# Two-layer interaction network: leftover products of layer 1 in batches of eight, other load times, a fifth operand buffer, and X5 and X4 behind X3 and X1

## The chip, the core and the metric

The kernel runs on one core of a Trainium2 chip. TensorE (PE in the profile, with its weight loads as PEld) multiplies matrices, VectorE (DVE), ScalarE (ACT) and GpSimd (POOL) do elementwise work, and SyncE (SP) and ACT issue transfers (DMA). The metric is the time of one execution in device microseconds (us). The kernel before took 2045.23 us, the median of five runs from 2044.97 to 2048.3.

## The reference

For each of 4096 rows there is x with 32 fields and 16 embedding places. A layer forms all products of its input's fields with the fields of x at each place, weighs them into 128 outputs, adds a bias and normalises each output over all rows and places.

```python
def _cin_layer(out, x, W, b, gamma, beta):
    h = jnp.einsum('rne,rfe->rnfe', out, x).reshape(r, -1, e)
    h = jnp.einsum('rce,oc->roe', h, W) + b[None, :, None]
    return _batchnorm(h, gamma, beta)

h1 = _cin_layer(x, x, W1, b1, g1, beta1)            # 32*32 products -> 128
out, direct1 = (h1[:, :64], h1[:, 64:])
direct2 = _cin_layer(out, x, W2, b2, g2, beta2)     # 64*32 products -> 128
return jnp.concatenate([direct1, direct2], axis=1).sum(axis=-1)
```

Everything is float32. The means and variances of layer 1 are needed before layer 2 can begin.

## The kernel before

**Sites and tiles.** A site is one row at one embedding place; there are 65536. They are cut into 128 tiles of 512 sites. Layer 1 goes tile by tile; layer 2 goes by 64 chunks, each of two tiles side by side.

**Layer 1, the products.** In layer 1 the product of fields i and j is the same as that of j and i, so 528 different products are enough. For each tile `load_main` (L282) loads two operands, a and b, of 512 KB each, and one VectorE instruction (`multiply_main`, L384) makes the products z, 128 partitions by four blocks of 512. TensorE weighs them in four matmuls with 128 partitions each (L428). Sixteen products are left over per tile, of fields that stand 16 apart. Those of eight tiles (a *group*, `GROUP`) are packed into one tile zr of 128 partitions: `load_rem` (L275) loads r, 512 KB per group, and `leftovers` (L371) multiplies. `add_leftovers` (L376) weighs them: four matmuls of 32 partitions each, one for each of four tiles, which use four different row strips of the array and so run at the same time. The 32 partitions of a strip hold the leftovers of two tiles; the weights at index 4 or 5 of `w1_sb` are zero on the other tile's rows. So zr serves two batches of four.

**Order in layer 1.** In the loop over 124 tiles (L401) a batch of leftovers stands ahead of the main matmuls of each tile t that is a multiple of four; it begins the accumulation of tiles t to t+3. Only the first batch comes after tile 1 and ends tiles 0 and 1. Below, *s* is t modulo 8. r is loaded at s = 4 and multiplied at s = 0. A finished tile goes through `finish` (L342), one tile late: ScalarE copies all 128 rows with the bias to e, rows 0 to 63 to `kept` (which goes to DRAM as layer 2's input h) and rows 64 to 127 to `ed`; VectorE takes statistics of e (L115) and, every second tile, sums ed (L364).

**Buffers.** a and b have four buffers each (`lpool`), z has four (`zpool`), r and zr have one each (`rpool`), PSUM has six banks for accumulators (`psum`) and two for small results and layer 2's factors (`factors`). The loads of tile t+4 wait until VectorE has multiplied tile t, and z of tile t+4 waits until TensorE is done with tile t.

**Side work of layer 1** hangs on tile numbers in the list `EARLY` (L205): every 24 tiles x of 16 chunks is loaded in two halves (`load_x`, L187, with a stride through the array xb), ScalarE negates two pieces, VectorE forms four pieces of differences (L199) and the result goes to DRAM. Layer 2's first operands are loaded at tiles 75 (b), 83 (bx) and 91, 99, 107 and 115 (a). The weights w2 are loaded at tile 6; `combine_weights` (L319) forms sums of them on VectorE.

**The end of layer 1.** The last four tiles (`ENDING`) are weighed in two halves of 64 outputs (L461): first the half that layer 2 needs for its statistics, then the other, while VectorE and ScalarE work out the scale and shift (L505 to L519, L537).

**Layer 2** takes each chunk in four stages of a form of Strassen's algorithm: seven products of blocks in place of eight. VectorE forms two products of a stage (L667), `multiply(z[:, 0::3], f1, b)` and then `multiply(z[:, 1:3], f2, bx)`, and one sum (t2); GpSimd forms a sum (L703) and two differences (t1 and t4 in one instruction, L714). A stage has fourteen matmuls, two at a time on the two halves of the columns, in the methods `x2`, `x54`, `x31` and `x67` of `Stage`. x54 needs GpSimd's differences and is taken one stage late: the loop (L856 on) issues x2, then x54 of the stage before (`waiting`), then x31 and x67.

**What sets the order.** The order on each engine is that of the program for layer 2 (`queue` chains the instructions) and, for layer 1, that of a scheduler which moves instructions of different tiles past each other within their dependencies. SP issues its loads in a fixed order: one that waits holds all behind it.

Of the kernel before, what the change touches and what calls it, by code (L numbers as in the profile page):

```python
# [38 lines left out]
FP = mybir.dt.float32  # L42
AF = mybir.ActivationFunctionType
ALU = mybir.AluOpType
AX = mybir.AxisListType

P = 128
# [3 lines left out]
T = 512  # L51
NC = HALF // T
NT = 2 * NC
# [3 lines left out]
WRAP = 48  # L57
# [10 lines left out]


@with_exitstack  # L70
def tile_cin(ctx: ExitStack, tc: tile.TileContext, xa, xb, xr, w1, w1m, w2, bn, out):
    nc = tc.nc

    const = ctx.enter_context(tc.tile_pool(name="const", bufs=1))
# [89 lines left out]
    def load_a(c, i):  # L164

        a = apool.tile([P, 2 * T], FP, tag="a", name="a")
        nc.sync.dma_start(a, hs[c][16 * i : 16 * (i + 1), :].unsqueeze(1).to_broadcast([16, 8, 2 * T]))
        return a

    def load_b(c):  # L170

        b = bpool.tile([P, 4, T], FP, tag="b", name="b")
        at = xb.offset + 2 * c * WRAP * T
        nc.sync.dma_start(b, bass.AP(xb.tensor, at, [[0, 16], [4 * T, 8], [1, 4 * T]]))
        return b
# [10 lines left out]

    def load_x(g, k):  # L187

        at = xb.offset + ((2 * DIFF * g + 1) * WRAP + 2 * k) * T
        nc.sync.dma_start(xs[:, k], bass.AP(xb.tensor, at, [[2 * WRAP * T, DIFF], [4 * T, 8], [1, 2 * T]]))  # L190

    def negate(part):
        x = xs[:, 0, part * T : (part + 1) * T]
# [10 lines left out]

    EARLY = []  # L205
    for g in range(NC // DIFF):
        at = 14 + 24 * g
        EARLY += [(at + 2 * k, lambda g=g, k=k: load_x(g, k)) for k in range(2)]
        EARLY += [(at + 12 + 2 * k, lambda k=k: negate(k)) for k in range(2)]
        EARLY += [(at + 16 + 2 * k, lambda k=k: difference(k)) for k in range(4)]  # L210
        EARLY += [(at + 23, lambda g=g: store_difference(g))]
    early = []
    EARLY += [(75, lambda: early.append(load_b(0))), (83, lambda: early.append(load_bx(0)))]
    EARLY += [(91 + 8 * k, lambda i=i: early.append(load_a(0, i))) for k, i in enumerate(STAGES)]
    loads = []

    def loaded(c):
# [43 lines left out]
    ss1 = const.tile([P, 2], FP, tag="ss1", name="ss1")  # L261

    with ExitStack() as one:
        lpool = one.enter_context(tc.tile_pool(name="lpool", bufs=4))
        rpool = one.enter_context(tc.tile_pool(name="rpool", bufs=1))
        opool = one.enter_context(tc.tile_pool(name="opool", bufs=2))
        kpool = one.enter_context(tc.tile_pool(name="kpool", bufs=3))
# [1 line left out]
        zpool = one.enter_context(tc.tile_pool(name="zpool", bufs=4))  # L269
        wpool = one.enter_context(tc.tile_pool(name="wpool", bufs=1))  # L270

        xs = xpool.tile([P, 2, 2 * T], FP, tag="x", name="xs")
        xd = xpool.tile([P, 2 * T], FP, tag="xd", name="xd")

        def load_rem(g):  # L275
# [87 lines left out]
        def sum_direct(c):  # L363
# [4 lines left out]
                ALU.add,  # L368
            )

        def leftovers(r):  # L371
            zr = rpool.tile([P, T], FP, tag="zr", name="zr")
            nc.vector.tensor_tensor(zr, r[:, :T], r[:, T:], ALU.mult)
            return zr

        def add_leftovers(t, zr, begun=0):  # L376

            for k in range(4):
                rows = slice(32 * k, 32 * (k + 1))
                nc.tensor.matmul(  # L380
                    pss[t + k], w1_sb[rows, 4 + t % GROUP // 4, :], zr[rows, :], start=k >= begun, stop=k < begun
                )

        def multiply_main(z, a, b, k):  # L384

# [14 lines left out]
        r = load_rem(0)  # L400
        for t in range(NT - ENDING):  # L401
            s = t % GROUP
            if s == 4 and t + 4 < NT:
                r = load_rem(t // GROUP + 1)
            if FIRST <= t + 1 < NT:
                main.append(load_main(t + 1))
            if s == 0 and t > 0:
                zr = leftovers(r)
            z = zpool.tile([P, 2, 2, T], FP, tag="z", name="z")
            if t < FIRST:  # L410
                for k in range(2):
                    for j in range(2):
                        product = multiply_chunk(z, *main[0], k, j)
            else:

                for k in (slice(0, 1), slice(1, 2)) if t == FIRST else (slice(0, 2),):
                    product = multiply_main(z, *main[0], k)
            main.pop(0)
            if t == FIRST - 1:
                with tc.issue_after(product.ins):  # L420
                    zr = leftovers(r)
            if s % 4 == 0:
                for k in range(4):
                    pss[t + k] = psum.tile([P, T], FP, tag="ps", name="ps")
            if s % 4 == 0 and t > 0:
                add_leftovers(t, zr)
            for m in range(4):
                nc.tensor.matmul(  # L428
                    pss[t],
                    w1_sb[:, m, :],  # L430
                    z[:, m // 2, m % 2, :],
                    start=t < FIRST and m == 0,
                    stop=t >= FIRST and m == 3,
                )
            if t == FIRST - 1:
                add_leftovers(0, zr, FIRST)
            if t > 0 and t < ending - 1:
                evicted = finish(t - 1)
            if t == 20:
                combine_weights()  # L440
                b1_swapped = const.tile([P, 1], FP, tag="b1s", name="b1_swapped")
                for x, y in ((low, high), (high, low)):
                    nc.scalar.activation(b1_swapped[x], b1[y], AF.Identity)
            if t == 0:
                continue
            with tc.issue_after(loads[-1].ins), tc.issue_after(product.ins), tc.issue_after(evicted.ins):
                if t == 12:
                    nc.vector.tensor_reduce(spread, select.rearrange("k i n f -> k (n f) i"), AX.X, ALU.max)
                if t == 14:
                    nc.vector.tensor_reduce(block, select.rearrange("k i n f -> k i (n f)"), AX.X, ALU.max)  # L450
                if t == 6:
                    nc.sync.dma_start(w2_sb, w2)
                for at, load in EARLY:
                    if t == at:
                        load()
# [19 lines left out]
        def add_leftovers_halves(banks, zr, direct, begun):  # L475

            for k in range(ENDING):
                rows = slice(32 * k, 32 * (k + 1))
                to = banks[k][half_of[(k + direct) % 2]]
                matmul(to, w1_sb[rows, 5, half_of[direct]], zr[rows, :], k not in begun, k in begun)  # L480

        zs = []
        for k in range(ENDING):
            if k + 1 < ENDING:
                main.append(load_main(ending + k + 1))
            zs.append(zpool.tile([P, 2, 2, T], FP, tag="z", name="z"))
            queue("dve", lambda: multiply_main(zs[k], *main.pop(0), slice(0, 2)))

        with tc.issue_after(lasts["dve"].ins):
            for t in (ending - 2, ending - 1):  # L490
# [365 lines left out]
    for c in range(NC):  # L856
# [3 lines left out]
        for k, i in enumerate(STAGES):  # L860
# [37 lines left out]
            if c == k == 0:  # L898
                stage.ordinary()
            elif (c, k) == (NC - 1, 3):  # L900
                stage.at_last(waiting)
            else:
                stage.x2()
                if waiting:
                    waiting.x54()
                stage.x31()
                stage.x67()
            if c > 0 or k > 0:
                waiting = stage
# [99 lines left out]
```

## Time and profile before

| | |
|---|---|
| median of five runs | 2045.23 us |
| the profiled execution | 2044.97 us |
| its span, first to last instruction | 2043.2 us |
| TensorE busy | 2026.8 us, 99% |
| VectorE busy | 1959.4 us, 96% |
| GpSimd busy | 1486.8 us, 73% |
| ScalarE busy | 1185.7 us, 58% |
| first main matmul of layer 1 | at 8.19 us |
| first matmul of layer 2 | at 490.38 us |
| last matmul of layer 2 starts | at 2030.18 us |

In the lines of a profile L428 is line 428 of the program. A float32 matmul shows as two instructions. A timeline line gives start and duration in us, engine, line, operation, the tile written and the tiles read, the shapes, and the number of instructions merged in it; in square brackets stands the engine's idle time just before it, and what ended it. A busy TensorE is not a TensorE at its peak, since matmuls overlap; what counts is the distance between their starts.

### The profile page before, as it was taken

The page shows a single profiled execution, that of the slowest core. Times are in us where ns is not written, and L with a number is a line of the kernel's source. Part 1 is how long each engine was busy: PE and PEld are TensorE (multiplying, and loading weights), DVE is VectorE, ACT ScalarE, POOL GpSimd, SP SyncE. Part 2 cuts the span into 40 slices and gives each one's busy share as a digit, 9 for nine tenths or more (in the row PEclk, how much of TensorE's full clock was granted, in tenths as well). Part 3 has the DMA queues.
Part 4 walks back from the last instruction along what each step waited for, and adds up shares of the span by engine and source line. Part 5 has one row for each costly group of instructions (what it writes and reads, how often), then busy time and mean ns, then how long its engine had stood idle before and what let it go on. Part 6 is the DMA issues. An engine that isn't in the chain of part 4 may idle for free.

```text
span 2043.2 us, 24467 instructions
## 1 busy us (share of the span) xinstructions
PE 2026.8 (99%) x8500; PEld 863.5 (42%) x8500; DVE 1959.4 (96%) x1521; ACT 1185.7 (58%) x1914; POOL 1486.8 (73%) x525
## 2 busy tenths in 40 slices
PE   9999999999999999999999999999999999999997
PEld 3444444443334444444444444444444444444443
DVE  8998988988999999999999999999999999999998
ACT  4555555554566666655665656556656565566564
POOL 0000000002999999999999999999999999999996
PEclk9999999999999999999999999999999999999998
DMA  9999999996777777777776677777766777777661
GB/s 391 373 353 370 347 361 370 359 374 189 176 178 175 176 175 180 192 174 183 179 176 168 172 175 176 178 181 177 176 167 173 175 173 184 179 176 176 168 163 42
DMA packets 112380, 440.70 MB, mean 216 GB/s; under 512 B 13056, under 2 KB 13056, under 8 KB 103808
## 3 DMA queue, kind: packets, MB, share of 16 engines
q1 hardware_dynamic: 105840, 418.43, 73.1%
q10 hardware_dynamic: 6416, 20.72, 2.7%
q8 instruction: 66, 1.08, 0.2%
q14 instruction: 58, 0.48, 0.1%
HBM read 417.07 MB, written 22.02 MB: 215 GB/s over the span
## 4 chain that ended last, share of the span: by engine, by line
PE 97%; DVE 1%; DMA 1%; issue 0%; ACT 0%; POOL 0%; DVEq 0%; ACTq 0%; POOLq 0%
PE x L698 73%; PE ps L428 21%; PE ps L380 2%; PE ps L461 1%; DVE zz L667 1%; DMA b<-in_xb 0%; DMA w1m_sb<-in_w1m 0%; DVE zz L672 0%; POOL t L714 0%; ACT f L659 0%; DVE d L934 0%; ACT u L659 0%; DVE both L662 0%; ACT both L659 0%; POOL t L703 0%
## 5 line engine op out<-in xcount | busy, mean ns | idle before, releaser
L714 POOL TENSOR_TENSOR t<-zz,t 128x2048 f32<-128x2048 f32 (+1 forms) x260 | 1163.9, 4477 | 20.7 <-DVE t L662 0.8
L698 PE MATMUL x<-t,s_sb 128*64 128x512 f32 x2040 | 958.3, 592 | 0.5 <-POOL t L714 0.5
L698 PE MATMUL x<-zz,s_sb 128*64 128x512 f32 x2048 | 933.1, 592 | 0.0
L698 PE MATMUL x<-zz,w_sb 128*64 128x512 f32 x2056 | 758.6, 592 | 0.0
L703 POOL TENSOR_TENSOR t<-zz 128x512 f32<-128x512 f32 x255 | 327.0, 1282 | 516.2 <-DVE zz L667 515.9
L667 DVE TENSOR_TENSOR zz<-f,bx 128x2048 f32<-128x2048 f32 x255 | 581.9, 2282 | 19.5 <-ACT f L659 19.5
L659 ACT ACTIVATE f<-a,keep 128x512 f32<-128x512 f32 x512 | 398.2, 778 | 342.7 <-DVE zz L667 294.7
L667 DVE TENSOR_TENSOR zz<-f,b 128x2048 f32<-128x2048 f32 x255 | 581.9, 2282 | 0.1
L698 PEld LDWEIGHTS x<-t,s_sb 128*64 128x64 f32 x2040 | 279.0, 137 | 498.6 <-issue 469.5
L698 PE MATMUL x<-t,w_sb 128*64 128x512 f32 x1020 | 479.3, 592 | 0.0
L428 PE MATMUL ps<-z,w_sb 128*128 128x512 f32 x992 | 434.7, 596 | 2.0 <-POOL w_sb L312 1.8
L698 PEld LDWEIGHTS x<-zz,s_sb 128*64 128x64 f32 x2048 | 279.7, 137 | 253.9 <-issue 246.3
L387 DVE TENSOR_TENSOR z<-a,b 128x2048 f32<-128x2048 f32 (+1 forms) x127 | 288.1, 2270 | 42.4 <-PE ps L428 27.8
L428 PEld LDWEIGHTS ps<-z,w_sb 128*128 128x128 f32 x992 | 185.7, 190 | 248.9 <-issue 230.7
L698 PEld LDWEIGHTS x<-zz,w_sb 128*64 128x64 f32 x2056 | 235.8, 137 | 124.5 <-issue 122.3
L659 ACT ACTIVATE b<-zz 128x512 f32<-128x512 f32 x255 | 152.4, 598 | 187.1 <-DVE zz L667 187.1
L352 ACT ACTIVATE e<-ps,bn_sb 128x512 f32<-128x512 f32 x124 | 85.2, 687 | 218.4 <-PE ps L428 182.2
L662 DVE TENSOR_TENSOR t<-zz,b 128x512 f32<-128x512 f32 x255 | 173.0, 678 | 0.4
L698 PEld LDWEIGHTS x<-t,w_sb 128*64 128x64 f32 x1020 | 139.4, 137 | 0.0
L596 ACT ACTIVATE unread<-e,center 128x512 bf16<-128x512 f32 x122 | 86.2, 707 | 0.0
L358 ACT ACTIVATE ed<-ps,bn_sb 64x512 f32<-64x512 f32 x124 | 84.8, 684 | 2.3
L115 DVE BATCH_NORM_STATS2 stats<-e 128x6 f32<-128x512 f32 x124 | 84.8, 685 | 0.0
(103 smaller groups left out, 866.0 us busy)
## 6 DMA issues: line engine op xcount, KB each, us to landing
a<-h SPq DMA_DIRECT2D x256, 512.0 KB, 4.5
b<-in_xb SPq DMA_DIRECT2D x64, 1024.0 KB, 9.0
a<-in_xa SPq DMA_DIRECT2D x127, 512.0 KB, 7.5
b<-in_xb SPq DMA_DIRECT2D x127, 512.0 KB, 8.2
bx<-in_xb SPq DMA_DIRECT2D x64, 512.0 KB, 8.9
bx<-x SPq DMA_DIRECT2D x64, 512.0 KB, 10.5
h<-kept ACTq DMA_DIRECT2D x64, 256.0 KB, 5.7
r<-in_xr SPq DMA_DIRECT2D x16, 512.0 KB, 9.3
```

The lines of the kernel that those rows point to most:

```text
L115: nc.vector.bn_stats(self.stats[:, self.at, :], h)
L352: nc.scalar.activation(e, ps, AF.Identity, bias=b1)
L358: done = nc.scalar.activation(ed[to, :], ps[KEEP:, :], AF.Identity, bias=b1[KEEP:])
L387: return nc.vector.tensor_tensor(z[:, k], a.rearrange("p (a t) -> p a t", a=2)[:, k].unsqueeze(2).to_broadcast([P, n, 2, T]), b.rearrange( ...
L428: nc.tensor.matmul(pss[t], w1_sb[:, m, :], z[:, m // 2, m % 2, :], start=t < FIRST and m == 0, stop=t >= FIRST and m == 3,)
L596: return nc.scalar.activation(unread, e[:, s], AF.Square, bias=center[:, s], accum_out=squares[:, s, c : c + 1])
L659: return queue("act", lambda: nc.scalar.activation(to, source, AF.Identity, **scale_bias))
L662: return dve(lambda: nc.vector.tensor_tensor(to, x, y, ALU.add))
L667: dve(lambda: nc.vector.tensor_tensor(z, a, b.rearrange("p (k q) t -> p k q t", k=2), ALU.mult))
L698: queue("pe", lambda: nc.tensor.matmul(self.of[x], w, b, start=start, stop=stop))
L703: queue("pool", lambda: nc.gpsimd.tensor_tensor(t2[:, 0], z[:, 1, 0], z[:, 0, 0], ALU.add))
L714: queue("pool", lambda: nc.gpsimd.tensor_tensor(t14[:, k, q], z[:, 2 + k.start : 2 + k.stop, q], twice[:, k, q], ALU.subtract))
```

## The change

1. **Leftovers.** At s = 0 two batches stand behind each other: first that of the four tiles just finished (s = 4 to 7 of the group before), which it *ends*, then that of the four tiles to come, which it *begins*. zr now holds the leftovers of tiles 8k-4 to 8k+3, so r is packed anew (17 pieces in place of 16), is loaded at s = 1 (and at tile 3), and the last four tiles get a product of their own.
2. **Banks and evictions.** Tiles with s = 6 and 7 use the two banks of `factors`; `finish` comes four tiles late in place of one.
3. **Loads.** x for the differences comes as one contiguous array, at tiles 8 and 11 (and every 24 on) in place of 14 and 16, into a buffer of `bpool`; b is loaded at tile 65, bx at 73, a at 88, 96, 104 and 112.
4. **Buffers.** a and b of layer 1 have five buffers.
5. **Layer 2.** In the stages k = 1 to 3 of a chunk x54 comes behind x31; at k = 0 it stays ahead.

```diff
-        at = xb.offset + ((2 * DIFF * g + 1) * WRAP + 2 * k) * T
-        nc.sync.dma_start(xs[:, k], bass.AP(xb.tensor, at, [[2 * WRAP * T, DIFF], [4 * T, 8], [1, 2 * T]]))
+        nc.sync.dma_start(xs[:, k], xd_in[2 * g + k])
...
-        at = 14 + 24 * g
-        EARLY += [(at + 2 * k, lambda g=g, k=k: load_x(g, k)) for k in range(2)]
+        at = 8 + 24 * g
+        EARLY += [(at + 3 * k, lambda g=g, k=k: load_x(g, k)) for k in range(2)]
...
-    EARLY += [(75, lambda: early.append(load_b(0))), (83, lambda: early.append(load_bx(0)))]
-    EARLY += [(91 + 8 * k, lambda i=i: early.append(load_a(0, i))) for k, i in enumerate(STAGES)]
+    EARLY += [(65, lambda: early.append(load_b(0))), (73, lambda: early.append(load_bx(0)))]
+    EARLY += [(88 + 8 * k, lambda i=i: early.append(load_a(0, i))) for k, i in enumerate(STAGES)]
...
-        lpool = one.enter_context(tc.tile_pool(name="lpool", bufs=4))
+        lpool = one.enter_context(tc.tile_pool(name="lpool", bufs=5))
...
-        xs = xpool.tile([P, 2, 2 * T], FP, tag="x", name="xs")
+        xs = bpool.tile([P, 2, 2 * T], FP, tag="bx", name="xs")
...
+        def bank(t):
+            pool, tag = (psum, "ps") if t % GROUP < 6 else (factors, "f")
+            return pool.tile([P, T], FP, tag=tag, name="ps")
+
+        def ends_with_leftovers(t):
+            return t % GROUP >= 4 or t < FIRST
+
-        def add_leftovers(t, zr, begun=0):
+        def add_leftovers(t, zr):
             for k in range(4):
                 rows = slice(32 * k, 32 * (k + 1))
-                nc.tensor.matmul(
-                    pss[t + k], w1_sb[rows, 4 + t % GROUP // 4, :], zr[rows, :], start=k >= begun, stop=k < begun
-                )
+                last = ends_with_leftovers(t + k)
+                w = w1_sb[rows, 4 + (t + 4) % GROUP // 4, :]
+                nc.tensor.matmul(pss[t + k], w, zr[rows, :], start=not last, stop=last)
...
-            if s == 4 and t + 4 < NT:
+            if s == 1 and t > 1 or t == 3:
                 r = load_rem(t // GROUP + 1)
...
-            if s % 4 == 0 and t > 0:
+            if s == 0 and t > 0:
+                add_leftovers(t - 4, zr)
                 add_leftovers(t, zr)
...
-            if t > 0 and t < ending - 1:
-                evicted = finish(t - 1)
+            if t >= ending - 2:
+                evicted = finish(t - 2)
+            elif t >= ending - 4:
+                for done in range(2 * t - ending, 2 * t - ending + 2):
+                    evicted = finish(done)
+            elif t >= 4:
+                evicted = finish(t - 4)
...
             queue("dve", lambda: multiply_main(zs[k], *main.pop(0), slice(0, 2)))
+            if k == 0:
+                zr = rpool.tile([P, T], FP, tag="zr", name="zr")
+                queue("dve", lambda: multiply_leftovers(zr, r))
...
                 stage.x2()
+                products = [stage.x31]
                 if waiting:
-                    waiting.x54()
-                stage.x31()
+                    products.insert(k > 0, waiting.x54)
+                for issue in products:
+                    issue()
                 stage.x67()
```

In the built program the number of instructions on TensorE is the same, 31 batches of four as before; fifteen pairs of them now stand behind each other. VectorE has one product zr more, SP one load of r more. The scheduler now puts VectorE's work of a group (tiles u0 to u7) in this order: the products z of u0 to u3, the statistics of the four tiles before (s = 4 to 7) with their two sums and the next zr among them, then z of u4 to u7, each followed by the statistics of u0 to u3. Before, each z was followed by the statistics of one tile. At the start SP issues the second load of r ahead of the loads of tile 4 (before, behind them), and VectorE has the second zr and a sum ahead of z of tile 4 (before, only the statistics of tiles 0 and 1). From tile 8 to tile 13 VectorE's order is: z8, z9, statistics of tiles 4 and 5, their sum, statistics of 6, z10, statistics of 7, z11, a sum, statistics of 8, z12, a reduction named spread, statistics of 9, a sum, zr, z13.

## What the prediction said

> **What bounds the kernel now.** I read the busy slices first, then the chain that ended last, then timelines around the places the change touches.
>
> ```profile
> PE   9999999999999999999999999999999999999997
> DVE  8998988988999999999999999999999999999998
> DMA  9999999996777777777776677777766777777661
> ```
>
> TensorE is full throughout. In layer 1 (slices 1 to 9 and half the tenth) the DMA engines are nearly full too, and VectorE is close. The chain decides which of them sets the end:
>
> ```profile
> 144.04 1.07 PE ps L380 x8
> 145.11 13.93 PE ps L428 x32
> 159.04 1.07 PE ps L380 x8
> ...
> 527.14 1498.50 PE x L698 x6980
> ```
>
> It runs on TensorE from 8.19 us to 486.9, with 15.00 us for each four tiles from 24 to 474, so no transfer and no VectorE wait reaches the end there; and on TensorE again from 527 to 2025.6. So only distances between matmul starts count. The reader must see those of one batch:
>
> ```profile
> 83.44 0.59 PE L428 MATMUL ps<-z,w_sb 128*128 128x512 f32 x1
> ...
> 83.96 0.31 PEld L380 LDWEIGHTS ps<-zr,w_sb 32*128 32x128 f32 x8 [0.76 <-ACT ed L358]
> 83.96 0.71 PE L380 MATMUL ps<-zr,w_sb 32*128 32x512 f32 x4
> ...
> 84.49 0.61 PE L380 MATMUL ps<-zr,w_sb 32*128 32x512 f32 x4
> 85.03 0.30 PEld L428 LDWEIGHTS ps<-z,w_sb 128*128 128x128 f32 x2 [0.76 <-DVE stats L115]
> 85.56 0.19 PEld L428 LDWEIGHTS ps<-z,w_sb 128*128 128x128 f32 x1 [0.24 <-issue]
> ```
>
> Matmuls of one kind start 0.429 us apart (83.01, 83.44). From the last main matmul to the batch it is 0.52, to the batch's second half 0.53, to the first main 0.54, to the second 0.53. No weights are loaded in the 0.52 before 83.96 and in the 0.54 before 85.03: when the kind changes, the load waits until the array is empty, and then delays its own matmul by 0.10. The excess over 0.429 is about 0.10 at each of the four steps, 0.41 in all; two halves of 0.43 and this make 1.27, and 32 x 0.429 + 1.27 = 15.00.
>
> **1. Leftovers, two batches together.** Fifteen pairs lose one set of changes. The unknown step is from the first batch's second half to the second batch's first half: same strips, other weights. The nearest row is 83.96 to 84.49: also same strips and other weights, all eight loads done within 0.31, and the 0.53 is the exposed 0.10 of the first half plus a plain 0.43. So I take 0.43 for the two added steps: a double batch costs 2.13 in place of 2 x 1.27, which is 0.41 less, **15 x 0.41 = 6.2 us less**. If each added step takes 0.53, as that row does at face value, 0.21 is saved, 3.1 us in all. Less than nothing is excluded, for no step in the trace is longer.
>
> The Trainium skill ("TensorE: Matmul & The Clock Gate", Part 3, The mechanism) speaks against this: a weight load overlaps running matmuls only when the row group differs, and here it is the same. By that rule the sum is the 3.1. The rows disagree: all four second loads fall under running matmuls of their own strips, so I stay with 6.2.
>
> **2. Does VectorE still keep ahead?** It may not wait for long now: the statistics of four tiles wait for one double batch. Call its start L. From rows: a product z takes 2.2 start to start, statistics 0.6, a sum 0.6, zr 0.6; ScalarE takes 1.98 a tile (e at 16.98 and 18.95), and e is ready 0.69 after its start. The first half-batch is done 1.17 after its start (83.96 + the 1.14). So the e of the four tiles are ready at L+1.9, 3.8, 5.8, 7.8 and the last ed at L+9.1. VectorE's queue: z of u3 until L+2.3, four statistics, two sums and zr, which end behind that ed at L+9.7. Then z of u4 until 11.9. TensorE needs it at L+1.94+0.10+4x3.43 = L+15.8: 3.9 us to spare (before it had about 9). Behind it z and statistics take 2.8 or 3.4 a tile against 3.43, so the lead is regained; differences (0.6 each, 2 a half group) leave over 2.5. Banks: u4's of the group before are free at L+9.1. I count **nothing** here. The loads: a group moves 8 x 1.05 + 0.52 + 4 x 0.26 = 10.0 MB in 29.6 us, 337 GB/s; the windows before show 399 (150 to 180 us), and the fifth buffer covers the 9.6 us in which no z ends. The differences' loads and layer 2's first loads add at most 2 MB to one group, within the 11.8 MB that 399 would carry.
>
> **3. The start.** Here the lead is small.
>
> ```profile
> 13.51 0.68 DVE L373 TENSOR_TENSOR zr<-r 128x512 f32<-128x512 f32 x1
> ...
> 19.64 1.28 DVE L115 BATCH_NORM_STATS2 stats<-e 128x6 f32<-128x512 f32 x2
> 20.84 2.27 DVE L387 TENSOR_TENSOR z<-a,b 128x2048 f32<-128x2048 f32 x1
> ...
> 10.98 0.54 SPq L294 DMA_DIRECT2D a<-in_xa  x1
> 11.56 0.60 SPq L294 DMA_DIRECT2D b<-in_xb  x1
> 14.22 0.34 SPq L279 DMA_DIRECT2D r<-in_xr  x1
> ```
>
> The second r waits for the first zr (14.2). It now stands ahead of tile 4's loads, which slip from 11 to 14.6 with all behind them, and land about one r later (512 KB at the 420 GB/s of full slices, 1.2 us), near 21. VectorE puts zr and a sum, 1.2, ahead of z4: 22.04 to 24.3. TensorE, with no batch at tile 4 now, wants it at 23.9: 0.5 late. Then L = 38.2; z8 and z9 are done by 40.0, statistics of 4, 5, 6 and a sum follow ScalarE until L+6.4 = 44.6, z10 46.8 (needed 47.1), then by the built order 0.6, z11, 1.2, z12, and 0.94 + 0.6 + 0.6 + 0.6 (spread, statistics, sum, zr) ahead of z13: ready 58.1, wanted 57.4. Together **1.2 us more**. Bounds: nothing (z4 and z13 just in time), and 2.4 if r and tile 4 land 1.2 later still (loads of 512 KB take 7.5 to 10.8 us). A gain is excluded: after 10.5 us no matmul of layer 1 was late.
>
> **4. The end of layer 1.**
>
> ```profile
> 474.11 2.29 DVE L387 TENSOR_TENSOR z<-a,b 128x2048 f32<-128x2048 f32 x1 [1.14 <-PE ps L428]
> ```
>
> Before, the product of tile 127 is done at 476.4, and TensorE takes it at 475.02 + 3.43 = 478.45. Now tile 120 is a group's u0: the queue of part 2, with a group's statistics (0.9), frees VectorE at L+10.0; z124, statistics, the new zr, z125, statistics and sum, z126, z127 end at L+21.3. TensorE is ready at L+15.87+1.02+3.43 = L+20.3. **1.0 us more**, and all that follows (statistics, keep, layer 2) shifts with it, since the tail of layer 1 on TensorE and VectorE's first layer 2 product meet at 490.3 as before. Bounds: 0 to 2 (one z more).
>
> **5. Layer 2.** What x54 costs now:
>
> ```profile
> 527.14 0.64 PE L698 MATMUL x<-t,s_sb 128*64 128x512 f32 x1 [0.48 <-POOL t L714]
> ```
>
> This start is 0.67 late (526.04 plus 0.43 is 526.47): GpSimd's difference ends at 527.1. Starts in layer 2 are otherwise 0.429 apart; I find about 0.5 more over all, around 612, 637 and 661, mostly x31 of k = 0 behind ScalarE, where nothing moves. x31, four pairs (1.72 us), moves ahead, so this wait goes. Late next: x54 of k = 0 in chunk 2, at 539.21, whose difference ends at 538.86. With TensorE 0.72 earlier it waits 0.43. **0.3 us less.** The price of the move is that x31 needs the second product 1.72 earlier: at 619.24 it had been done (617.1) for 2.14, the least after the first stages; 0.42 stays, 0.13 after the 0.3. Starts 0.1 behind a product are seen (490.38 after 490.29). Bounds: 1.2 less (all late starts go) to 0.5 more.
>
> x in one piece and the earlier loads end no wait that TensorE sees: nothing. Gain excluded because the chain has none; cost up to 0.5 within part 3's bound.
>
> **Sum:** -6.2 + 1.2 + 1.0 - 0.3 = -4.3 on the profiled execution's 2044.97 (span 2043.2 and 1.8 around it), which is 0.26 below the median. So 2045.23 - 4.3 = **2040.9 us**.
>
> **Rivals.** (a) The added steps of a double batch are not covered, 0.53 each: -3.1 + 1.9 = **2044.0 us**; the leftovers then do little of what the change names. For it: 0.53 is the only such step in the profile. Against: its 0.10 belongs to the first half. (b) Start and end cost nothing and all late starts of layer 2 go: -6.2 - 1.2 = **2037.8**. For it: VectorE's idle before z, 41.7 us in layer 1. Against: it lies in steady stretches. (c) Slower: transfers become the bound. Loads go out only as z end; a group has 9.6 us without one. If the queues run dry for 5 of these, 10.0 MB must pass in 24.6 us, 407 GB/s; where only 378 passes (330 to 360 us), a group takes 1.8 longer, fourteen of them 25: 2040.9 + 25 = **2066**. It decides from 3.2 us of dry queues a group (29.6 less 10.0 MB at 378). For it: DMA share 0.92 to 1.03 in layer 1. Against: five buffers, and queues that fall behind do not run dry.
>
> **Numbers.** Forecast 0.50, (a) 0.15, (b) 0.20, (c) 0.10 (from 2 us a little to 25), 0.05 for a layer 2 where x31 becomes late, some 2042. The forecast's own range is 2039.3 to 2042.5. Leaving out most of (c) and the far half of (b): 2038.0 to 2044.6. 0.2% is 4.1 us, about what a measurement of this kernel can tell from no change; 2041.1 is that line. Of the forecast a bit over half lies below it: faster 0.27 + 0.20 = 0.47; within 0.23 + 0.15 + 0.05 = 0.43; slower 0.10.
>
> **What would show it.** Chain: pieces of L393 x16 with 1.07 + 2 x 0.43 = 1.93 us, between stretches of x64, and 29.6 us per eight tiles; 29.8 speaks for (a). A wait of a main matmul for VectorE near 24 and 58 and before the last z, half to one us each; none speaks for (b). More than 29.7 in mid layer 1, with SP or DMA ending VectorE's waits, speaks for (c). In layer 2, the start behind POOL near 526 gone and one near 537 in its place. Wrong would be any batch of L393 that waits for ScalarE's banks.

## The result and the profile after

| us | before | after |
|---|---|---|
| median | 2046.34 (42 runs, 2044.97 to 2048.30) | 2041.95 (22 runs, 2041.04 to 2043.87) |
| profiled execution (its span) | 2044.97 (2043.2) | 2041.28 (2039.6) |
| first main matmul | 8.19 | 8.35 |
| eight tiles of mid layer 1 | 30.00 | 29.59 |
| first batch of the last four tiles to layer 2's first matmul | 16.38 | 17.33 |
| layer 2, first matmul to last | 1539.79 | 1539.81 |

The ratio of the times is 0.998, 95% interval 0.9974 to 0.9986: **0.2% less time**, 4.4 us between the medians and 3.7 between the two traces. Predicted were 2040.9 us, within 2039.3 to 2042.5, and 4.3 us less than before. The prediction's own line of 0.2%, 4.1 us, lies between the two measured differences.

The slices of the page after, as shown of before:

```profile
PE   9999999999999999999999999999999999999997
DVE  8998898989999999999999999999999999999997
DMA  9998999996777677777767677777776777776761
```

At this grain nothing has moved: TensorE full, transfers near full in layer 1. The chain that ended last (start, us, what) tells more:

```profile
58.38 10.54 PE ps L441 x24
68.92 1.93 PE ps L393 x16
...
98.51 1.93 PE ps L393 x16
...
537.14 1484.88 PE x L720 x6916
```

A double batch is one piece of sixteen, 1.93 long, and the next begins 29.59 later (98.51 - 68.92), where before it was 2 x 15.00. In the one that begins at 98.44, the weights of the second batch's two halves (the rows at 98.98 and 99.41; each holds the loads of four strips) are loaded while matmuls on the same strips run:

```profile
98.44 2.00 PE L393 MATMUL ps<-zr,w_sb 32*128 32x512 f32 x16
98.98 0.20 PEld L393 LDWEIGHTS ps<-zr,w_sb 32*128 32x128 f32 x4 [0.22 <-issue]
99.41 0.20 PEld L393 LDWEIGHTS ps<-zr,w_sb 32*128 32x128 f32 x4 [0.23 <-issue]
```

Layer 1 is on TensorE without a break from 58.38, not from 24, so something ahead of 58.38 is late; and the break of layer 2 that stood at 527.14 stands at 537.14. TensorE's timeline shows the two late starts of layer 1:

```profile
24.46 14.00 PE L441 MATMUL ps<-z,w_sb 128*128 128x512 f32 x32 [0.28 <-DVE z L398]
...
58.38 1.95 PE L441 MATMUL ps<-z,w_sb 128*128 128x512 f32 x4 [0.63 <-DVE z L398]
```

The bracket is idle time after the modelled end of the matmul before; the cost is taken from start to start. At 24.46 that is 0.87 - 0.43 = 0.44, and 0.10 more on the next step, since the next weights were not loaded yet: 0.54 for z4. At 58.38 it is 0.79 + 0.08 = 0.87 for z13. VectorE ahead of z13:

```profile
53.22 1.03 DVE L467 TENSOR_REDUCE spread<-select 64x128 f32<-64x512 f32 x1
...
55.36 0.68 DVE L373 TENSOR_TENSOR zr<-r 128x512 f32<-128x512 f32 x1
55.96 2.28 DVE L398 TENSOR_TENSOR z<-a,b 128x2048 f32<-128x2048 f32 x1
```

With statistics and a sum in the place left out, that is the row of four that the prediction laid ahead of z13; z13 ends at 58.2 and TensorE wanted it at 57.6. At the end of layer 1 the last two products end at 474.78:

```profile
470.30 4.48 DVE L398 TENSOR_TENSOR z<-a,b 128x2048 f32<-128x2048 f32 x2
```

The double batch before began at 453.56, so this is L+21.2 (predicted L+21.3). TensorE doesn't stand still for it: the two column halves of tiles 126 and 127 run as pairs, and it began tile 126's half alone, so one matmul (two starts) at each end of that stretch was left without its partner. Those 48 took 11.47 instead of 10.52: 0.95.

From the traces: -6.16 for the batches, +1.41 at z4 and z13, +0.95 at the end, +0.02 in layer 2, and +0.16 for a first matmul that came later for w1's load, which the change doesn't touch: **-3.62**, and layer 2's last matmul starts 3.61 earlier.

### The profile page after: what moved, and what is told of

It reads as the page before. It is cut to its first block, busy times and chain, and to the rows that moved or that the text cites. A ratio compares the mean times of both kernels' runs of the same rounds, so it can differ in the third digit from the quotient of the medians.

```text
span 2039.6 us, 24500 instructions
## 1 busy us (share of the span) xinstructions
PE 2023.1 (99%) x8500; PEld 893.7 (44%) x8500; DVE 1956.6 (96%) x1522; ACT 1189.8 (58%) x1914; POOL 1487.4 (73%) x525
## 4 chain that ended last, share of the span: by engine, by line
PE 96%; DMA 2%; DVE 1%; issue 0%; POOL 0%; ACT 0%; SPq 0%; DVEq 0%; ACTq 0%; POOLq 0%
PE x L720 75%; PE ps L441 19%; PE ps L393 1%; PE ps L480 1%; DMA r<-in_xr 1%; DMA b<-in_xb 0%; DMA h<-kept 0%; DMA w1m_sb<-in_w1m 0%; POOL t L736 0%; DVE z L398 0%; DVE zz L689 0%; SPq L295 0%; DVE d L959 0%; ACT u L681 0%; POOL t L725 0%
## 5 line engine op out<-in xcount | busy, mean ns | idle before, releaser
L720 PE MATMUL x<-zz,s_sb 128*64 128x512 f32 x2048 | 955.6, 592 | 0.0
L720 PE MATMUL x<-t,s_sb 128*64 128x512 f32 x2040 | 927.4, 592 | 0.2 <-POOL t L736 0.2
L720 PE MATMUL x<-zz,w_sb 128*64 128x512 f32 x2056 | 729.7, 592 | 0.0
```

The costliest lines, as they stand in the source:

```text
L720: queue("pe", lambda: nc.tensor.matmul(self.of[x], w, b, start=start, stop=stop))
```

## The experiments

Each edit is to the kernel after. "Trace" is the time from the first main matmul to layer 2's last against the kernel after's 2018.22. Four of the traces hold a drop of TensorE's clock near 10 us; it is told in its place below (experiment 11).

Two things help to compare medians. They were taken at different times: before's own median, taken beside them, was 2046.23 for experiments 1 to 4, 2046.06 for 6 to 9, 2045.72 for 5, 10 and 11, and 2045.22 for 12. And each execution's mean granted clock is on record to three places. A drop of 3.4 us to 0.50 takes 0.0008 off it, so it tells roughly which executions held one. Of the kernel after's 23 executions (the traced one among them), 7 have 0.998, with a median of 2041.28; 14 have 0.997, with 2042.12; two have 0.996. Of before's 31 beside experiments 1 to 4, 13 have 0.998, with 2045.13, and 17 have 0.997, with 2046.69.

### 1. The double batches taken apart

```diff
-            return t % GROUP >= 4 or t < FIRST
+            return t % GROUP >= 4 or t < FIRST or t % GROUP == 0
...
-                last = ends_with_leftovers(t + k)
+                last = ends_with_leftovers(t + k) or (t % GROUP == 0 and k == 0)
...
                 add_leftovers(t - 4, zr)
-                add_leftovers(t, zr)
...
-            if t == FIRST - 1:
-                add_leftovers(0, zr)
+            if t == FIRST - 1 or (s == 0 and t > 0):
+                add_leftovers(t // GROUP * GROUP, zr)
```

> Against the kernel after: only the double batch of leftovers is taken apart again; the two batches of a group stand on either side of tile t's main matmuls; loads, buffers and layer 2 stay. Theory (every single batch costs four start-to-start steps about 0.10 us longer than 0.429, two of them going in and two coming out, and a double batch saves one set): 15 x 0.41 = 6.2 us more, less up to 0.4 where tile 13's product is then less late; eight tiles of layer 1 take 30.00 us instead of 29.59, and the pieces of leftovers in the chain are x8 again. So 5.8 to 6.2 more, about 2047.9. Rival (the gain comes from the loads or the fifth buffer, which take the edge off transfers): within 1 us of the kernel after, 2042.

Median 2047.01 (2046.13 to 2048.30), against before 1.0006 (0.9997 to 1.0016); trace +5.76. The chain of this kernel:

```profile
69.97 1.07 PE ps L393 x8
...
75.74 24.23 PE ps L440 x56
...
105.74 24.23 PE ps L440 x56
```

Eight tiles take 30.00 again (105.74 - 75.74). So 15 x 0.41 = 6.15 back; with it go 0.95 at the end and 0.42 of z13's wait, as TensorE arrives later there, and the start is 1.0 longer by a lowered clock: 6.15 - 0.95 - 0.42 + 1.0 = 5.8. The theory holds; with everything else of the change in place and only the pairs of batches split, the gain is gone.

### 2. X5 and X4 ahead of X3 and X1 again

```diff
-                    products.insert(k > 0, waiting.x54)
+                    products.insert(0, waiting.x54)
```

> Against the kernel after: the products of X5 and X4 stand ahead of X3 and X1 again in every stage. Theory (the move takes one late start of 0.67 us away and makes another, 0.5, and a third, 0.2, behind ScalarE's copy of e, so it is worth nothing): 0.0, within 0.1 in the trace; the start behind GpSimd in stage 6, near 522, comes back with about 0.67, and X3's start of the next chunk is on time. Rival (the move gains the 0.3 us that the prediction gave it): 0.3 more between the first and the last matmul of layer 2.

Median 2041.16; layer 2 takes 1539.79, against 1539.81 after and 1539.79 before. Its late start is back near 523:

```profile
523.39 0.64 PE L720 MATMUL x<-t,s_sb 128*64 128x512 f32 x1 [0.43 <-POOL t L736]
```

In the kernel after that one is gone, and in its place (TensorE, then ScalarE):

```profile
535.20 0.64 PE L720 MATMUL x<-t,s_sb 128*64 128x512 f32 x1 [0.15 <-POOL t L736]
...
537.14 0.64 PE L720 MATMUL x<-zz,s_sb 128*64 128x512 f32 x1
```

```profile
536.50 0.59 ACT L681 ACTIVATE e<-x 64x512 f32<-64x512 f32 x1
```

x54 of chunk 2's first stage is late by 0.35 and 0.05, and x31 behind it, at 537.14, by 0.18 and 0.05: it waits for the copy e, which ends at 537.09. That copy ends 50.33 us after layer 2's first matmul in both kernels. So the move gains nothing: the theory. (The median lies 0.8 under the kernel after's, but 8 of these ten executions have a mean clock of 0.998, and their median, 2041.12, is 0.2 under that of the kernel after's.)

### 3. Four operand buffers

```diff
-        lpool = one.enter_context(tc.tile_pool(name="lpool", bufs=5))
+        lpool = one.enter_context(tc.tile_pool(name="lpool", bufs=4))
```

> Against the kernel after: four pairs of operand buffers instead of five. Theory (the products lead TensorE by at least 3.5 us in mid layer 1, and the loads reach VectorE with time to spare): 0, within 0.3 us, with VectorE's waits for DMA going from 1 us back towards the 14 of before. Rival 1 (the fifth buffer is what keeps the double batches fed): TensorE waits in mid layer 1, 2 us or more. Rival 2 (fewer loads at once early on land sooner, so the start gains): up to 0.5 us less, seen as a smaller wait at tile 4.

Median 2044.34 (2043.05 to 2046.61); trace +2.98. My theory fell, and rival 1 holds. Five groups of mid layer 1 are longer than 29.59, by 1.16, 0.34, 0.07, 0.36 and 0.38, 2.31 in all; VectorE waits 22 us for loads there, against 0.2 in the kernel after. The rest of the 2.98 is the clock at the start (1.10 more up to the first batch, 0.41 less in z4's wait).

### 4. The due times of before, x still in one piece

```diff
-        at = 8 + 24 * g
-        EARLY += [(at + 3 * k, lambda g=g, k=k: load_x(g, k)) for k in range(2)]
+        at = 14 + 24 * g
+        EARLY += [(at + 2 * k, lambda g=g, k=k: load_x(g, k)) for k in range(2)]
...
-    EARLY += [(65, lambda: early.append(load_b(0))), (73, lambda: early.append(load_bx(0)))]
-    EARLY += [(88 + 8 * k, lambda i=i: early.append(load_a(0, i))) for k, i in enumerate(STAGES)]
+    EARLY += [(75, lambda: early.append(load_b(0))), (83, lambda: early.append(load_bx(0)))]
+    EARLY += [(91 + 8 * k, lambda i=i: early.append(load_a(0, i))) for k, i in enumerate(STAGES)]
```

> Against the kernel after: layer 2's loads and those of x go out at the due times of before (x still in one piece). Theory (no wait that TensorE sees is ended by them): 0, within 0.3 us. Rival (spread loads keep transfers from piling up at the end of layer 1, where the products are late): 0.5 us or more, as a longer wait before the last product of layer 1 or before layer 2's first.

Median 2041.28 (2040.19 to 2042.52); trace +0.49, from two parts that neither side expected. One group, from 364 us, is 1.37 longer: with the DMA share full, ScalarE issued a store at 372.55, 3.8 us after the eviction before it, and its third eviction of the group came at 373.10, so that the statistics, and z behind them, came late. What held the store the trace doesn't tell (the profile names a matmul that had long been done). And z13's wait of 0.87 is gone: in this kernel's order VectorE makes that zr ahead of z11, and statistics and a sum stand behind z13. So the new due times cost 0.87 at tile 13 and save 1.37 later, in this trace. The times don't bear out a saving: at equal mean clock these executions are shorter than the kernel after's (0.998: 2040.85 against 2041.28; 0.997: 2041.34 against 2042.12). So with five buffers the new due times aren't shown to gain anything, and seem to cost about half a us.

### 5. The double batches alone

Edits 2, 3 and 4 together, and x for the differences in pieces as before:

```diff
-        nc.sync.dma_start(xs[:, k], xd_in[2 * g + k])
+        at = xb.offset + ((2 * DIFF * g + 1) * WRAP + 2 * k) * T
+        nc.sync.dma_start(xs[:, k], bass.AP(xb.tensor, at, [[2 * WRAP * T, DIFF], [4 * T, 8], [1, 2 * T]]))
...
-        xs = bpool.tile([P, 2, 2 * T], FP, tag="bx", name="xs")
+        xs = xpool.tile([P, 2, 2 * T], FP, tag="x", name="xs")
```

> The double batches alone: against the kernel after, four operand buffers, the due times of before, the differences' x in pieces again, and X5 and X4 first. Theory (the double batches pay 6.2 us whatever else is there, and what the other parts of the change do is to keep the loads from being late for them: with four buffers TensorE waited 2.4 us in mid layer 1, with the old due times 1.4): TensorE's waits in mid layer 1 are 2 to 4 us, periods of 29.59 elsewhere, so 2043 to 2045. Rival (the two waits come from how one order of instructions happened to fall, and don't add): 1 us or less of waits, 2041 to 2042.

Median **2049.72** (2045.95 to 2052.05), 1.0019 of before (1.0010 to 1.0028): slower than before. Trace +6.94. The theory's sign holds and its size doesn't; the waits are more than the sum of those that experiments 3 and 4 brought singly. (x in pieces was not run by itself.) All groups take 29.59, the one with tile 13 too, except one of 36.71 (7.12 more, 0.87 less at tile 13 and 0.68 more at the start by the clock make the 6.9). VectorE's waits for loads (line waited for: us in total, times, longest), in the stretch 60 to 465 us; first the kernel after, then this one:

```profile
DVE z L398 <- DMA b<-in_xb: 0.2, 1, 0.2
```

```profile
DVE z L399 <- DMA b<-in_xb: 24.0, 18, 3.6
```

In the long group:

```profile
345.67 7.13 PE L442 MATMUL ps<-z,w_sb 128*128 128x512 f32 x16 [1.19 <-DVE z L399]
356.53 8.80 PE L442 MATMUL ps<-z,w_sb 128*128 128x512 f32 x16 [3.73 <-DVE z L399]
```

The two waits cost 1.35 and 3.89 from start to start, and then sixteen matmuls take 8.80 instead of 7.13. Windows of one microsecond (PE, PEld, DVE, ACT, POOL busy with counts, then TensorE's granted clock, DMA share, GB/s) show why:

```profile
357.00:358.00 1.00, 1.00 (x2) 0.33 (x1) 1.00 (x1) 0.97 (x2) 0.00 (x0) 0.50 0.42 123
358.00:359.00 1.00, 1.00 (x3) 0.46 (x2) 1.00 (x1) 0.99 (x3) 0.00 (x0) 0.50 0.92 242
359.00:360.00 1.00, 1.00 (x3) 0.48 (x2) 1.00 (x3) 0.53 (x2) 0.00 (x0) 0.50 0.97 311
```

After the wait the granted clock is 0.50 for 3.4 us, which costs another 1.77. So 1.35 + 3.89 + 1.77 = 7.0 of the group's 7.1; the step behind the first wait is 0.10 longer. The DMA share stands at 1.01 to 1.03 from 300 to 355 us: the queues aren't dry, the loads come in too late. In that stretch 353 GB/s pass, against 370 in the kernel after, so transfers that were slower may have a part in it besides the missing buffer; no run takes the two apart.

### 6. The wait at tile 4

```diff
-            if s == 1 and t > 1 or t == 3:
+            if s == 1 and t > 1 or t == 4:
```

> Against the kernel after: the second load of r goes out one tile later, behind tile 4's loads instead of ahead of them. Theory (the new wait of 0.54 us at tile 4 comes from r standing ahead of tile 4's loads in SP's queue and from zr and a sum standing ahead of z4 on VectorE): that wait goes, 0.5 us less; the wait at tile 13, 0.87, stays, since VectorE is pinned there by the statistics behind ScalarE. Rival (tile 4 is late because of all loads together, whatever their order): no change at tile 4, 0. Second rival: r itself is then late for the double batch at tile 8, a new wait of over 0.5 at the first x16.

Median 2041.89. From the first batch to the second 22.25 instead of 22.41: z4 is in time, and z5, which now has zr ahead of it, is 0.28 late, with 0.10 more on the step behind it. A wait handed on to the next product; tile 13's stays at 0.87.

### 7. The wait at tile 13

```diff
-                if t == 12:
+                if t == 28:
...
-                if t == 14:
+                if t == 30:
```

> Against the kernel after: the two reductions that spread the selection for layer 2 (0.94 and about 0.1 us) are made at tiles 28 and 30 instead of 12 and 14. Theory (tile 13's product is late because VectorE has 0.94 us of spread, besides statistics, a sum and zr, between z12 and z13, in the stretch in which it hasn't its lead yet): the wait of 0.87 us at tile 13 goes or is at most 0.1, 0.8 us less, and no wait takes its place at tile 28, where the lead is over 3.5 us. Rival (VectorE is behind there because it waits for ScalarE, and catches up only from tile 15 on): the next product, 14 or 15, is late by nearly as much, 0.3 us less at most.

Median 2040.42 (2040.19 to 2041.63); trace -0.85. The second period is 29.59 instead of 30.46, and no wait comes at tile 28: as the theory had it.

### 8. The end of layer 1: zr ahead of the statistics

```diff
+            if t == ending - 3:
+                zr = leftovers(r)
...
-            if k == 0:
-                zr = rpool.tile([P, T], FP, tag="zr", name="zr")
-                queue("dve", lambda: multiply_leftovers(zr, r))
```

> Against the kernel after: the last zr (0.6 us) is made while VectorE still has its lead, ahead of the last group's statistics, and not between z124 and z125. Theory (the end of layer 1 is set by VectorE's queue up to z127, of which that zr is a part): z127 ends up to 0.6 earlier, the end of layer 1 gains 0.5 us, from 16.82 to about 16.3 us between the last batch of leftovers and the end of tile 127. Rival (the pair that TensorE takes apart at tile 126 costs its two steps whatever the product's time): at most 0.1.

Median 2041.28 (2040.48 to 2042.03); the end of layer 1 takes 16.73 instead of 17.33, 0.60 less, as the theory had it. The 48 matmuls take 10.87; 0.35 stays.

### 9. The end of layer 1: evictions behind the last products

```diff
-                evicted = finish(t - 2)
+                pass
...
-            for t in (ending - 2, ending - 1):
+            for t in range(ending - 4, ending):
                 evicted = finish(t)
```

> Against the kernel after: the evictions and statistics of tiles 120 and 121 stand behind the last four products of layer 1 instead of ahead of z126 and z127. Theory: z127 ends some 2.3 us earlier, so that TensorE never waits for it and takes the two column halves of tile 126 as a pair; the end of layer 1 gains 0.95 us, from 16.82 to 15.87 us, the time before; what VectorE leaves for later (two statistics and sums, 1.8) stands ahead of layer 2's first product and may take up to 0.9 of it back, where layer 2's first matmul then comes late. Rival 1 (the end is set by the banks that ScalarE frees): 0, since the evictions of tiles 120 and 121 come later, a new wait for ScalarE before the leftovers of the last tiles. Rival 2: VectorE is the bound of the whole seam between the layers, so what z127 gains, layer 2's first product loses: 0 in all.

Median 2042.71: slower, 18.18 instead of 17.33. The products are early, and TensorE waits for a bank:

```profile
478.52 4.36 PE L480 MATMUL ps<-z,w_sb 128*64 128x512 f32 x16 [0.88 <-ACT kept L525]
```

ScalarE had nothing to do from 466.7 to 473.8. It waited for VectorE's statistics, which now stand behind the last product; then it evicts tiles 122 and 123, until 477.8, ahead of the half of tile 124 whose bank TensorE needs. This is near rival 1's mechanism, dearer than it said and in another place: the statistics can't be moved there, since ScalarE waits for them. A sum can (experiment 10).

### 10. Three repairs together

Edits 7 and 8, and only the sum of chunk 60 (0.6 us) behind the last product:

```diff
-            if half == 1:
+            if half == 1 and t != ending - 3:
                 sum_direct(c)
...
         with tc.issue_after(lasts["dve"].ins):
+            sum_direct(ending // 2 - 2)
             for t in (ending - 2, ending - 1):
```

> Three repairs of the kernel after at once: the spread of the selection made at tiles 28 and 30, the last zr made ahead of the last group's statistics, and the sum of chunk 60 made behind the last product. Theory (each takes a stretch of VectorE from ahead of a late product): 0.87 less at tile 13, 0.60 + 0.35 less at the end of layer 1 (from 17.33 to 16.38 us between the last batch and layer 2's first matmul, the time that two other kernels show there); together 1.8 less than the kernel after where TensorE's clock isn't lowered at the start, 2039.5, and a median near 2040. Rival (the end of layer 1 is held by ScalarE's evictions of tiles 122 and 123 once VectorE isn't late): 16.73, as with the zr alone, so 1.5 less.

Median **2039.45** (2039.21 to 2039.56, five runs), 0.9968 of before (0.9956 to 0.9981). The second period is 29.59 and the end 16.38, the time before: both terms of the cost at tile 13 and at the end are gone, as the theory had it. All five have a mean clock of 0.998, and lie 1.83 under the kernel after's with that clock: 0.87 + 0.95.

### 11. More matmuls ahead of the first product

```diff
-BEGIN = 3
+BEGIN = 4
```

> Against the kernel after: eight matmuls on constants ahead of the first product instead of six, so that TensorE stands idle for less time (6.6 to 8.4 us from the span's start in most traces) before the first main matmul. Theory (in some executions TensorE's granted clock is 0.50 for 2.5 to 4 us from about 9 to 13 us, which costs up to 1.4 us; the idle stretch ahead is what brings it): no dip in any execution, so the times of ten executions lie together near 2041.2, and the median is 0.5 to 0.7 less than the kernel after's 2041.95. Rival 1 (the dip has nothing to do with that idle stretch): medians alike, with two groups of times about 1 us apart as before. Rival 2 (the additional matmuls run into the first main matmul): up to 0.4 us more.

Why this was tried: the traces of experiments 1, 3, 5 and 8 hold a stretch of half clock near 10 us. That of experiment 3:

```profile
9.00:10.00 1.00, 1.00 (x3) 0.41 (x2) 1.00 (x2) 0.00 (x0) 1.00 (x1) 0.50 1.04 426
...
12.00:13.00 1.00, 1.00 (x3) 0.38 (x2) 1.00 (x3) 0.00 (x0) 0.00 (x0) 0.87 1.05 430
```

It makes the way to the first batch 1.1 to 1.4 us longer, of which 0.4 comes back at tile 4. With eight matmuls the ten executions lie from 2040.90 to 2041.42, with a median of 2041.19; with six the 22 lie from 2041.04 to 2043.87, with 2041.95. That is 0.76 less in the median and nothing in the trace, which holds no drop in either. Of the 0.76, 0.62 is what before's own median differs between the two sessions (2045.72 against 2046.34), so the medians alone don't show the theory. The spread fits it: none of the sixteen executions with eight matmuls, here and in experiment 12, lies more than 0.6 above the lowest of its kernel, and with six every kernel but that of experiment 10 has some that lie more than a us above. But those five lie within 0.35, and no execution with the drop was traced in the kernel after itself. So that eight matmuls keep the drop away is likely, not shown.

### 12. All repairs

Experiments 10 and 11, with r loaded at tile 6, so that zr stands behind z4, z5 and z6:

```diff
-            if s == 1 and t > 1 or t == 3:
+            if s == 1 and t > 1 or t == 6:
```

> The three repairs of the run before last (spread late, zr in the gap, the sum of chunk 60 behind the last product), the eight matmuls on constants, and the second load of r three tiles later, so that on VectorE its zr stands behind the products of tiles 4, 5 and 6. Theory: no matmul of layer 1 is late after the first tiles (the wait of 0.3 to 0.5 us at tile 4 goes and none comes at tile 5, 6 or 8), so 22.00 us between the first batch of leftovers and the second, 29.59 for each group after it and 16.38 at the end; 0.3 us less than with the three repairs alone: 2039.1, ten executions within 0.6 us. Rival (moving zr back only hands the wait on to the next product, as it did when r went out one tile later: 0.54 at tile 4 became 0.28 at tile 5): 0.1 less at most, 2039.4.

Median **2038.96** (2038.80 to 2039.34, six runs), 0.9968 of before (0.9956 to 0.9980). That is 3.0 less than the kernel after's median, taken in another session; at a mean clock of 0.998 it is 2.3, and between the traces 2.5. TensorE's layer 1 up to the fourth batch:

```profile
8.29 7.70 PE L441 MATMUL ps<-z,w_sb 128*128 128x512 f32 x16 [1.25 <-POOL w_sb L313]
...
16.98 20.87 PE L441 MATMUL ps<-z,w_sb 128*128 128x512 f32 x48
37.78 2.00 PE L393 MATMUL ps<-zr,w_sb 32*128 32x512 f32 x16
39.71 27.73 PE L441 MATMUL ps<-z,w_sb 128*128 128x512 f32 x64
```

No bracket after the first line, up to the end of layer 1. Against the trace of after: 0.54 at tile 4, 0.87 at tile 13, 0.95 at the end, 0.1 elsewhere, 2.46 of the 2.48 us between the two executions.

## Why the prediction was right, and where it was not

**The batches: right.** Each added step costs 0.429 (0.409 from the last strip of one half to the first strip of the next, and 0.020 in which the four strips start one after the other), so a pair of batches saves 0.41, and fifteen of them 6.16 of the predicted 6.2. Experiment 1 takes exactly this away. Rival (a), 0.53 a step, is out, and with it, for this case, the rule of the Trainium skill that the prediction weighed ("TensorE: Matmul & The Clock Gate", Part 3, The mechanism): weights for strips in use were loaded under running matmuls (98.98 and 99.41 above).

**Mid layer 1: right in the sum, and its reason incomplete.** "I count nothing here" holds for the kernel after: z of a group's fifth tile is ready 3.5 to 3.8 us early from the third group on (predicted 3.9), and no matmul waits. But the average rate, 337 GB/s against 399, says little: experiments 3 and 5 move the same bytes, and TensorE waits 2.3 and 5.2 us. A fifth buffer is what made the difference in experiment 3. "x in one piece and the earlier loads end no wait that TensorE sees: nothing" speaks of before, where they do nothing; with the double batches and four buffers they are, all together, part of what keeps the loads in time (experiment 5), while with five buffers the earlier due times gained nothing (experiment 4). Late loads are what rival (c) named, though not by its reason, queues that run dry: the share was full. With the cover they cost nothing, and without any of it 7.1 us in one group, more than the whole gain.

**The start: right in place, 0.2 too small.** z4 0.54 (0.5), z13 0.87 (0.7): both omitted the 0.1 of the weight load that a late start uncovers. Experiments 6 and 7 confirm the causes, zr and a sum ahead of z4, the spread ahead of z13. The later loads of tile 4 had no part: VectorE began z4 without a wait for them. That the earlier load of x had a part in z13's order was not foreseen (experiment 4).

**The end: right, 0.95 for 1.0.** The product ends at L+21.2. The price came otherwise than thought: TensorE takes the half that is ready by itself and loses the pair at both ends, so that the sizes agree so well is in part luck.

**Layer 2: wrong, 0.0 for "0.3 us less".** The failing step is the search for what is late next. It found x54 of chunk 2 (0.43 predicted, 0.40 measured), but not x31 behind it, which in the kernel before had 0.2 to spare to ScalarE's copy: with TensorE earlier by 0.72 - 0.40 = 0.32, it costs 0.18 and 0.05 on the next step. ScalarE's and VectorE's row sets that start in both kernels, at 50.3 us after layer 2's first matmul. Two steps of 0.05 more, at 561.72 and 585.80, take the rest, and the late start that stood at 613.18 before comes 122.80 us after layer 2's first matmul in both kernels. So a gain ahead of it would most likely have been taken back there.

**The sum and the medians.** The traces give -3.6 for the predicted -4.3: 0.3 from layer 2, 0.2 from the start, and 0.16 from the first matmul. That the medians differ by 4.4, so near to 4.3, is luck. They differ by 0.7 more than the traces, since before's traced execution is its lowest, 1.4 below its median, and after's is 0.7 below. The mean clock tells most of the rest: at 0.998 the two kernels' medians differ by 3.85 (2045.13 and 2041.28), near the traces. The executions with 0.997 are 1.56 longer before and only 0.84 longer after; the drop's 0.4 that comes back at tile 4 would explain half of that. That drops at the start are the whole of it wasn't shown.

## What to carry to other kernels

- Where TensorE is full, count the steps at which the kind of matmul changes: here four steps of 0.10 us. Standing like beside like saved 0.41 each time, and without that the rest of the change together saved nothing (experiment 1: 1.0006 of before).
- An edit that bunches work takes away slack that other engines lived on. Its price isn't in any wait of the profile before; take the covers away one by one and all together, for their loss together (7.1 us in one group, 1.8 of it by the clock) was more than that of two of them singly (2.3 and 1.4), in one trace of each.
- Where a wait is removed, look for the next late start on every engine that feeds the same one, and at the matmuls behind it too, by their margin before.

## What the runs showed of the hardware

**The granted clock can fall after a pause, and then for 3.4 us.** What the windows lack to 1.00, divided by 0.50, gives the time at 0.50: 3.40 (experiment 3), 3.42 (experiments 1 and 5), 3.40 (experiment 8). After the pause of 3.73 us in experiment 5 it fell 0.4 us after TensorE had begun again. Ahead of the first matmul a pause of 1.61, 1.90, 2.13 or 2.51 us had it, and pauses of 1.67 and 1.84 had not, so the length alone doesn't decide; below 1.6 it was never seen in these traces (ends of matmuls are modelled). The clock records that lie in the traces show what may: in all four the fall comes 3.41 us after the rise that the matmuls on constants had brought (at 6.39 and 9.80 in experiment 1, 5.44 and 8.85 in 3, 5.33 and 8.74 in 5, 6.46 and 9.87 in 8), and the second fall of experiment 5 comes 344.75 us, 101 such stretches, after the clock had risen again. So the clock seems to be judged in stretches of 3.41 us, by what TensorE did in each; how much it must do isn't shown. The Trainium skill ("TensorE: Matmul & The Clock Gate", Part 1, What's actually happening) gives some 3.4 us for an idle window that lowers the clock and for a busy one that raises it again. The second agrees with the rows; as a length of pause the first doesn't, since 1.61 us sufficed once.

**A late start costs more than its wait.** The load of the next weights isn't done under the matmul before, and the step after the late one is 0.08 to 0.10 longer as well (z4, z13, and x54 and x31 of layer 2 with 0.05).
